# Joining the weighing with the next half group's scores, norms and stores by half groups, and a new load order, in a planned four-layer graph kernel

## The chip, the cores and the metric

One core of one Trainium2 chip. The metric is the time of one execution in microseconds (us), the median of several on the device. All runs used here of one kernel agree within about 0.2%. TensorE is the matmul engine, DVE the vector engine, ACT the scalar engine, GpSimd (POOL in the profile) the fourth; PSUM is where TensorE writes. "One group" is four pairs of graphs, 512 nodes; there are 16 groups.

## The reference, cut to what matters

```python
# x (128, 64, 256), adj (128, 64, 64) holds 0 and 1 only, nodemask (128, 64); all float32
h = relu(layernorm(x));  x = x + attention_0(h, adj)    # 8 heads; where(adj > 0, scores, -9e15)
h = relu(layernorm(x));  x = x + attention_1(h, adj)    # scores + log(adj + 1e-6)
h = relu(layernorm(x));  x = x + gru(h, adj, nodemask)  # 5 steps, each: m = h @ weight[l]
                                                        # agg = (adj != 0)^T m;  h = GRU(agg, h)
h = relu(layernorm(x));  x = x + gated(h, adj)          # theta, norm by degree, gate, elu
```

## The kernel before

The kernel does not issue its instructions as they are written. Each is recorded with an assumed cost, an engine and its operands; a small planner then fixes the order of every engine's instructions at build time, as a list scheduler with a clock of its own:

```python
AFTER = {"PE": 210, "DVE": 125, "ACT": 45, "POOL": 90, "SP": 2500}   # ns from an end to its user
TO_PE = 120
AHEAD = 1.2
...
    @contextmanager
    def strand(self, base, span=1.0):       # gives the ops recorded inside keys base .. base + span
...
    def run(self):                          # cut: takes the op that can start first, by key, within
        ...                                 # a horizon of AHEAD; knows the port that DVE and GpSimd share
```

Attention works on half a group. Its two narrow blocks on TensorE use 64-wide tiles of the array: the scores (s) and the weighing of the values (o). They are recorded far apart:

```python
        def scores():                       # 8 matmuls, stationary operand 128x64
            for i in range(2):
                ps = pss[i].tile.rearrange("p (h k) -> p h k", h=HEADS)
                for c in range(2):
                    for gp in range(2):
                        t0 = i * P + gp * NODES
                        nc.tensor.matmul(ps[gp * NODES : (gp + 1) * NODES, c * 4 : (c + 1) * 4, :],
                                         qT[:, c, t0 : t0 + NODES], k_exp[:, c, :, t0 : t0 + NODES],
                                         start=True, stop=True)
        pe(1970, scores, [qT, k_exp], pss, holds=es)
        # cut: softmax on DVE, ACT, GpSimd; transposes of the weights (aT)
        pe(1180, weigh, [v_exp, *aTs], [po], holds=[oT])   # 16 matmuls, stationary operand 128x64
        # cut: oT copied by DVE, y = oT @ Wo, x += y
```

The recurrence (five steps, matmuls gb, gc, nb, nc and agg) is a chain; TensorE fills its waits with the attention of the next group ("front") and the last layer of the group before ("back"). That rests on these strands:

```python
    for g in range(n_groups):
        xt, h, ht, A, adjT, norm = held
        with plan.strand(g - 0.1, 1.05):
            h = gru(h, ht, A, str(g))
        if g + 1 < n_groups:
            with plan.strand(g + 0.1):
                held = front(g + 1)
        with plan.strand(g + 1.1, 0.6):
            back(g, xt, h, adjT, norm)
```

## Time and profile before

| | before |
|---|---|
| time, median | 2737.6 us (2737.26 to 2738.7, 3 runs) |
| profiled span, granted clock | 2738.0 us, 0.994 |
| TensorE idle from 200 to 2590 us | 2.2 us |
| one group in the steady state | 164.69 us |

The last row is how I read the steady state: each group has one group of four transposes named adjT, and in the list of matmuls by time they start at 755.43, 920.11, 1084.81, 1249.49 us, so 164.69 us apart.

### The profile page before, as it was taken

The numbers are of one execution on the slowest core, as the hardware profiler recorded it, in microseconds if no ns is written. First come the engines' busy times: TensorE is split into PE (matmuls) and PEld (weight loads), VectorE is DVE, ScalarE is ACT, GpSimd is POOL, SyncE is SP. The second block draws the span as 40 slices with busy tenths as digits, with TensorE's granted clock in tenths as the row PEclk, the third lists the DMA queues.
The fourth block names the chain that finished last, engine by engine and source line by source line (L and its number), as shares of the span: only waits on it lengthen the run. The fifth ranks groups of instructions, "written<-read, shape, count | busy, mean of one in ns | idle before, by whom it ended". The sixth has DMA issues, their size and how long they took to land.

```text
span 2738.0 us, 41144 instructions
## 1 busy us (share of the span) xinstructions
PE 2687.4 (98%) x15593; PEld 2244.2 (82%) x15593; DVE 1977.9 (72%) x4401; ACT 1410.1 (51%) x2743; POOL 764.0 (28%) x820
## 2 busy tenths in 40 slices
PE   8899999999999999999999999999999999999996
PEld 5688888888888888888888888888888888888884
DVE  4676687777777777777777777777777777777766
ACT  4445455455555545455455555555455455554542
POOL 5332232232332323232232332322222232322211
PEclk9999999999999999999999999999999999999998
DMA  3000000000000000000000000000000000000000
GB/s 122 5 1 1 1 17 5 1 16 1 17 5 10 8 1 20 1 16 1 1 20 1 17 1 8 13 1 16 1 16 1 1 17 1 16 1 1 9 8 8
DMA packets 31401, 27.70 MB, mean 10 GB/s; under 512 B 9234, under 2 KB 30948, under 8 KB 31204
## 3 DMA queue, kind: packets, MB, share of 16 engines
q1 hardware_dynamic: 31204, 25.08, 2.9%
q8 instruction: 123, 2.02, 0.3%
q14 instruction: 74, 0.61, 0.1%
HBM read 16.69 MB, written 8.39 MB: 9 GB/s over the span
## 4 chain that ended last, share of the span: by engine, by line
PE 95%; DVE 3%; ACT 1%; issue 1%; DMA 0%; POOL 0%; SPq 0%; POOLq 0%; DVEq 0%; ACTq 0%
PE gb L679 20%; PE gc L679 15%; PE nb L679 10%; PE nc L679 8%; PE agg L712 5%; PE s L528 4%; PE y L584 4%; PE gate L930 4%; PE q L473 4%; PE v L504 4%; PE k L473 4%; PE o L573 2%; PE hT L419 2%; PE aT L557 2%; PE lnT L419 2%; PE f L924 2%
## 5 line engine op out<-in xcount | busy, mean ns | idle before, releaser
L782 POOL TENSOR_TENSOR s0n<-h,s0n 128x512 f32<-128x512 f32 x80 | 108.1, 1352 | 718.8 <-ACT s0n L779 718.8
L679 PE MATMUL gb<-Th,w_hh 128*128 128x256 f32 x960 | 247.9, 381 | 1.8 <-DVE s22g L743 1.1
L679 PE MATMUL gb<-Ta,gv 128*128 128x256 f32 x960 | 247.7, 380 | 0.9 <-DVE Ta L722 0.8
L551 POOL TENSOR_TENSOR e<-e,ssum 128x512 f32<-128x512 f32 x128 | 139.5, 1101 | 307.8 <-DVE ssum L550 305.3
L743 DVE TENSOR_TENSOR s0g<-gc,ug 128x512 f32<-128x512 f32 x80 | 55.3, 692 | 215.5 <-PE gc L679 215.5
L679 PEld LDWEIGHTS gb<-Th,w_hh 128*128 128x128 f32 x960 | 176.8, 190 | 32.8 <-issue 10.0
L679 PEld LDWEIGHTS gb<-Ta,gv 128*128 128x128 f32 x960 | 178.2, 190 | 24.4 <-DVE Ta L722 1.7
L650 POOL TENSOR_TENSOR Th<-h 128x256 f32<-128x256 f32 x160 | 134.4, 844 | 216.5 <-PE nb L679 79.4
L717 ACT ACTIVATE agg<-agg 128x512 f32<-128x512 f32 x160 | 95.3, 595 | 182.0 <-DVE Ta L722 127.1
L650 POOL TENSOR_TENSOR Th<-h,Th 128x256 f32<-128x256 f32 x160 | 123.4, 771 | 233.7 <-DVE h L796 120.9
L772 ACT ACTIVATE s0g<-s0g,b_rz 128x512 f32<-128x512 f32 x160 | 110.6, 714 | 138.6 <-DVE s0g L743 138.5
L712 PEld LDWEIGHTS agg<-adjblk,ht 128*128 128x128 f32 x1280 | 164.3, 191 | 10.0 <-ACT ht L424 3.7
L712 PE MATMUL agg<-adjblk,ht 128*128 128x128 f32 x1280 | 169.8, 276 | 0.0
L679 PE MATMUL gc<-agg,gv 128*128 128x256 f32 x640 | 165.3, 381 | 0.0
L679 PE MATMUL gc<-h,w_hh 128*128 128x256 f32 x640 | 164.5, 379 | 0.0
L409 POOL TENSOR_TENSOR rstd<-pw,mhalf 128x4 f32<-128x4 f32 x64 | 65.4, 1022 | 300.9 <-DVE pw L408 300.9
L473 PE MATMUL q<-hT,w_L_gnn_Wq 128*128 128x256 f32 x512 | 146.0, 388 | 1.6 <-DVE hT L427 1.6
L446 DVE TENSOR_SCALAR xn<-x,mv,rstd 128x256 f32<-128x256 f32 x256 | 109.8, 461 | 51.0 <-POOL rstd L409 42.8
L679 PE MATMUL nb<-Th,w_hh 128*128 128x256 f32 x480 | 143.0, 380 | 0.0
L679 PE MATMUL nb<-Ta,gv 128*128 128x256 f32 x480 | 142.8, 379 | 0.0
L504 PE MATMUL v<-w_L_gnn_Wv,hT 128*128 128x256 f32 x512 | 138.4, 380 | 0.0
L473 PE MATMUL k<-hT,w_L_gnn_Wk 128*128 128x256 f32 x512 | 137.4, 381 | 0.0
(161 smaller groups left out, 6864.7 us busy)
## 6 DMA issues: line engine op xcount, KB each, us to landing
x<-in_x_dram SPq DMA_DIRECT2D x16, 512.0 KB, 3.8
out_dram<-x SPq DMA_DIRECT2D x16, 512.0 KB, 2.8
adjq<-in_adj_dram SPq DMA_DIRECT2D x8, 256.0 KB, 2.9
gv<-in_L_gnn_weight_dram SPq DMA_DIRECT2D x5, 256.0 KB, 5.6
w_ih<-in_L_gnn_w_ih_dram SPq DMA_DIRECT2D x2, 384.0 KB, 6.0
w_hh<-in_L_gnn_w_hh_dram SPq DMA_DIRECT2D x2, 384.0 KB
w_L_gnn_Wo<-in_L_gnn_Wo_dram SPq DMA_DIRECT2D x2, 256.0 KB, 4.2
w_L_gnn_Wq<-in_L_gnn_Wq_dram SPq DMA_DIRECT2D x2, 256.0 KB
```

The costliest lines, as they stand in the source:

```text
L419: nc.tensor.transpose(ps[:, i * P : (i + 1) * P], src_at(i), ident.tile)
L446: vec2(400, lambda p=p, i=i, xn=xn: nc.vector.tensor_scalar(xn[:, i, :], xt[:, p, :], mv[:, p, 0:1], rstd[:, p : p + 1], op0=ALU.subtract, ...
L473: pe(mm(256), lambda c=c, kc=kc: nc.tensor.matmul(ps[:, c * HALF : (c + 1) * HALF], wt[:, kc, c * P : (c + 1) * P], hT[:, kc, :], start=kc ...
L504: pe(mm(256), lambda i=i, kc=kc: nc.tensor.matmul(pv[:, i * D : (i + 1) * D], hT[:, kc, i * P : (i + 1) * P], w["v"][:, kc, :], start=kc = ...
L528: nc.tensor.matmul(ps[gp * NODES : (gp + 1) * NODES, c * 4 : (c + 1) * 4, :], qT[:, c, t0 : t0 + NODES], k_exp[:, c, :, t0 : t0 + NODES], ...
L551: pool(1090, lambda e=e, z=z: nc.gpsimd.tensor_tensor(e.tile, e.tile, z[:, :, None].to_broadcast(shape), op=ALU.mult), [e, z], [e])
L584: pe(mm(256), lambda i=i, c=c: nc.tensor.matmul(py[:, i * D : (i + 1) * D], oT[:, i, c, :], w["o"][:, c, :], start=c == 0, stop=c == 1), [ ...
L650: pool(790, lambda: nc.gpsimd.tensor_tensor(T[:, i, :], x(), y(), op=ALU.subtract), reads, [(T, i)])
L679: nc.tensor.matmul(bank_[:, col * HALF : (col + 1) * HALF], at(g, n), rhs(), start=first and j == 0, stop=True, skip_group_check=True)
L712: nc.tensor.matmul(ps[:, p * P : (p + 1) * P], ht[:, p, c * P : (c + 1) * P], A[:, p, :], start=True, stop=True)
L772: sca(act(n, 1), lambda k=k, col=col: nc.scalar.activation(wide(g_v, k), src_at(k), AF.Tanh, bias=b_rz[:, col : col + 1], scale=0.5), [src ...
L930: pe(mm(512), lambda kc=kc, s=s, pg=pg, hT=hT: nc.tensor.matmul(pg.tile, hT[:, kc, s], w_th[:, kc, :], start=kc == 0, stop=kc == 1), [hT, ...
```

## The change

Its intent: leave the narrow form of the array less often, by issuing one half's weighing directly ahead of the next half's scores; start sooner, by loading x first; fill the prologue with two groups' attention in turns; shorten the tail by half groups. The diff, cut to its core:

```diff
-            vec(345, ... bn_stats(st[:, p, :], xt[:, p, :]) ...        # norms: four tiles, one power
+    def norm_relu_t(xt, half, dst, access, writes, name, by_token=None):  # two tiles, one power each
...
-            transposed(dst, access, xn, ..., half == 1, writes, relu=True)  # half 0 on DVE, half 1 on ACT
+        transposed(dst, access, xn, ..., True, writes, relu=True)           # both on ACT
...
+        if waiting:
+            weigh_last, reads, po_last, oT_last, finish_last = waiting.pop()
+
+            def both():
+                weigh_last()
+                scores()
+
+            pe(2900, both, [*reads, qT, k_exp], [po_last, *pss], holds=[oT_last, *es])
+            finish_last()
+        else:
+            pe(1970, scores, [qT, k_exp], pss, holds=es)
...
-        pe(1180, weigh, [v_exp, *aTs], [po], holds=[oT])
+        waiting.append((weigh, [v_exp, *aTs], po, oT, finish))     # the last one of a group is flushed
...
-                nc.sync.dma_start(rows.tile[r0 : r0 + n, :], ...)       # bias rows, nodemask
+                nc.scalar.dma_start(rows.tile[r0 : r0 + n, :], ...)
+        plan.add("ACT", 2600, fill_rows, [], [rows], lat=2500)
+        load_x(0)                                                        # ahead of adj and weights
...
-    with plan.strand(-1.0):
-        held = front(0)
+    with plan.strand(-1.0):
+        for g in (0, 0, 1, 0, 1, 0):
+            next(parts[g])                                              # one half-layer each
...
-            with plan.strand(g + 0.1):
-                held = front(g + 1)
-        with plan.strand(g + 1.1, 0.6):
-            back(g, xt, h, adjT, norm)
+            with plan.strand(g - 0.1, 0.9):
+                for _ in parts[g + 1]:
+                    pass
+        with plan.strand(g + 1.1, 0.5):
+            back(g, xt, h, adjT, norm)                                  # itself by halves, stores too
```

## The prediction

> **What bounds the kernel now.** I read the page's busy shares first, then the busy times cut into stretches, then TensorE's matmuls in order of time, then the chain of waits at both ends. From the page of the kernel before:
>
> ```profile
> PE 2687.4 (98%) x15593; PEld 2244.2 (82%) x15593; DVE 1977.9 (72%) x4401; ACT 1410.1 (51%) x2743; POOL 764.0 (28%) x820
> ...
> PE   8899999999999999999999999999999999999996
> ```
>
> TensorE is busy 98%; the next engine, DVE, 72%. The digits say that TensorE's idle time lies in the first two and the last of 40 slices. Busy times in stretches that I chose at events of the trace (first norm transpose, first recurrent step, steady state, last group's recurrence, tail), TensorE alone (busy us, count, granted clock, DMA share, GB/s):
>
> ```profile
> 0.00:13.06 13.06, 2.42 (x5) 1.00 0.66 210
> 13.06:120.40 107.34, 97.24 (x549) 0.95 0.18 55
> 120.40:200.00 79.60, 76.20 (x452) 1.00 0.00 1
> 200.00:2590.00 2390.00, 2387.83 (x14032) 1.00 0.02 7
> 2590.00:2699.40 109.40, 104.02 (x506) 1.00 0.02 6
> 2699.40:2738.00 38.60, 19.67 (x56) 0.72 0.04 14
> ```
>
> From 200 to 2590 us TensorE is idle 2.2 us of 2390. There nothing but less TensorE work shortens the program; faster DVE, GpSimd or DMA is worth nothing. All other idle time is 10.6 + 10.1 + 3.4 + 5.4 + 18.9 = 48.4 us, 1.8% of the span, and much of it (the first load, the last chain) can't go. So even a perfect removal of idle time would stay under 2%, and that limits this prediction more than anything else.
>
> The second source is inside the busy time. TensorE's matmuls in order of time in the steady state (start, us, line, count; each matmul of the source stands as two):
>
> ```profile
> 731.75 0.60 PE L557 MATMUL aT<-ident,e 128*128 128x128 f32 x4
> 732.18 1.06 PE L712 MATMUL agg<-adjblk,ht 128*128 128x128 f32 x8
> 733.17 1.95 PE L528 MATMUL s<-kexp,qT 128*64 128x256 f32 x16
> 735.05 0.65 PE L557 MATMUL aT<-ident,e 128*128 128x128 f32 x4
> 735.54 0.60 PE L679 MATMUL nb<-agg,gv 128*128 128x256 f32 x2
> 735.97 1.03 PE L679 MATMUL gc<-agg,gv 128*128 128x256 f32 x4
> 736.93 1.15 PE L573 MATMUL o<-aT,vexp 128*64 128x64 f32 x32
> 738.01 0.70 PE L679 MATMUL nc<-agg,gv 128*128 128x256 f32 x2
> 738.55 1.03 PE L504 MATMUL v<-w_L_gnn_Wv,hT 128*128 128x256 f32 x4
> ```
>
> Read the starts, not the durations. Four matmuls of 256 columns normally take 0.86 us from start to start and two take 0.43. The four (gc) ahead of the weighing (o) take 736.93 - 735.97 = 0.96, and the two (nc) after it 738.55 - 738.01 = 0.54. So 0.10 us is lost on entering and 0.11 on leaving. For the scores (s): agg takes 0.99 where eight take 0.89 elsewhere (0.10 lost), and the transposes after it 0.49 where four take 0.43 (0.06 lost). Only s and o have a 128*64 stationary operand; all else has 128*128. None of this shows as idle.
>
> **What the Trainium skill says.** "TensorEngine Tiling (Array Packing)", Key Properties: "Changing tiling mode (not just tile) drains the TensorE". The trace agrees in sign and gives the size, about 0.1 us per change. "TensorE: Matmul & The Clock Gate", Part 1 (What's actually happening), says that an idle array falls to half clock until it has been busy for a window of about 3.4 us. The trace agrees: the first eight q matmuls took 3.62 us where a warm eight take 1.89, and in 75 to 100 us, after waits of 2.6 us and less, the mean granted clock was 0.81. "DMA: Bandwidth & Descriptors", Anatomy of one DMA, gives about 2.0 us fixed cost. Here the first load, 256 KB of adj issued at 0.73, let DVE start at 3.69: 2.96 us, no contradiction.
>
> **Part 1, weighing joined with the next scores.** The instruction orders of the two builds show 128 narrow blocks on TensorE before (64 s, 64 o, never adjacent), and 80 after: 48 joined, 16 s and 16 o alone. (A group has four half-layers; the last weighing of each group is flushed alone.) Counts of matmuls per kind are the same. Each join removes one leaving and one entering: 0.06 to 0.11 plus 0.10, say 0.20 us. 48 x 0.20 = **9.6 us**. As TensorE is full where most of them lie, I count all of it. The planner's own constants imply 0.25 per join (12 us).
>
> **Part 2, x first.** Before, x was the ninth load issued (4.29 us) and DVE's statistics began at 9.48; then 1.73 us of statistics for four tiles, 0.17 for adding epsilon, 1.03 for the power on GpSimd, 0.42 for the first normalisation, first transpose at 13.06:
>
> ```profile
> 9.48 1.41 DVE L439 BATCH_NORM_STATS2 st<-x 128x6 f32<-128x256 f32 x4 [2.92 <-DMA x<-in_x_dram]
> ...
> 11.53 1.03 POOL L409 TENSOR_TENSOR rstd<-pw,mhalf 128x4 f32<-128x4 f32 x1 [6.58 <-DVE pw L408]
> ...
> 13.06 1.22 PE L419 MATMUL lnT<-ident,xn 128*128 128x128 f32 x4 [4.36 <-DVE xn L446]
> ```
>
> After, half of x (256 KB) is the first load on its queue, so by the adj load's example it is there at about 3.7. Statistics of two tiles take about 0.9, power and its input 1.3, two normalisations 0.73: first transpose at about 6.7, **6.3 us earlier**. The bias rows move to ACT's queue: six issues of 0.23 to 0.64 us (2.1 us) and 2.1 to landing put the small transpose of them at about 5.2, as before, so it does not hold the first norm. Weights wanted first (Wq, Wk) follow x directly.
>
> **Part 3, two groups' attention in turns, weight folding spread.** Between 13 and 120 us TensorE idles 10.1 us and loses 0.05 x 107 = 5.4 us to the lower clock: 15.5 us in all. The largest waits are a normalisation (1.9 and 0.7), a softmax of group 0 that nothing filled (2.6) and a key placement behind it (0.4). Group 1's scores now stand between group 0's, and the GpSimd folds (20 + 4 adds of 1 us) move behind. But the new order runs dry of folding matmuls after the second layer's first half, and GpSimd stays busy. I count 40%: **6 us**, and 1.5 of the 3.4 us idle in 120 to 200.
>
> **Part 4, the tail by halves.** Today the last group's norm waits for both halves of h. After, the half that is ready first (h at 2703.5 by today's clock) goes through transposes (1.1 us), two residuals, statistics of two tiles and its own power while the other half's last update runs. On DVE these are interleaved, so I get the first transposes at about 2709.9 for 2712.07 today. From there DVE sets the pace: a tile takes 0.48+0.42+0.48+0.43+0.43+0.29+0.42+0.42 = 3.37 us of it and today's tiles follow each other by 3.07 to 3.49, which the change does not alter. So 2.2 us, and about 0.5 for a last store of 256 instead of 512 KB: **2.7 us**.
>
> **Part 5, what it adds.** Norms by halves double the powers: 64 more of 1.02 us on GpSimd (764 to about 830 of 2738 us) and move 64 PSUM evictions of 0.68 us from DVE to ACT as 0.59. Both engines have room and nothing of it is on the path in the steady state: 0. Stores and loads in halves move the same bytes in 32 more transfers, hidden: 0. The joined block needs three PSUM banks of four at once and both operands ready; I add 1.5 us for waits that this makes.
>
> Sum: 9.6 + 6.3 + 6 + 1.5 + 2.7 - 1.5 = 24.6 us. 2737.6 - 24.6 = **2713.0 us**, 0.9% less.
>
> **Rivals.** (a) The join becomes a wait: scores can't start before the last weighing's transposed weights are evicted, and three banks of four are held. For it: the order is fixed at build time, so a misplaced block stalls TensorE each time; 48 stalls of 0.4 us take back the whole of part 1 and half of part 3: about 2726. Against it: the same planner left 2.2 us idle in 2390, so its costs are good. (b) The load order starves the fold: the folding matmuls now stand between the first q, k and v and need the GRU weights by about 10 us; 2.5 MB must land first, and the first 25 us moved 280 GB/s (9 us). A late one costs 2 to 4 us and a cold clock: 2717. (c) The prologue works fully: all 15.5 us of part 3 and 12 us of joins return: about 2701. (d) GpSimd becomes the limit in the prologue, as it now has 24 folds, 12 norms and the softmax scalings of two groups: part 3 gives nothing, 2719. I hold the middle for likelier than either end.
>
> **Range and chances.** The rivals span 2701 to 2726; I widen by a little: 2700 to 2726. A gain of over 2% needs under 2682.8, 54.8 us less: more than all idle time plus the joins' 9.6 could give with a tail that must keep most of its 39 us; 3%. A loss of over 2% needs 55 us of new waits on a full TensorE: 1%.
>
> **What would show it.** Joins: o followed at once by s in the matmuls' order, without 0.1 us around them, and the steady stretch shorter by 0.6 us per group with as little idle time. Start: first norm transpose near 6.7. Prologue: idle and clock loss up to the first recurrent step down from 15.5 to about 9. Tail: last recurrent matmul to end 36 instead of 38.6. Wrong if: TensorE's waits on ACT's aT or on a bank grow by over 5 us in the steady stretch, the fold matmuls wait on a DMA, or a join saves other than 0.2 us.

## More of the kernel before

The few waits of that stretch, as the view of waits has them (waiting matmul, what it waited for: us in total, times, longest):

```profile
PE q L473 <- DVE hT L427: 0.8, 1, 0.8
PE nb L679 <- DVE h L427: 0.8, 1, 0.8
PE gate L930 <- DVE oT L579: 0.7, 1, 0.7
```

None of these three repeats: they belong to the first and last groups.

## The result, and the profile after

The changed kernel takes 2727.13 us (2725.76 to 2728.55, 4 runs) against 2737.43 in the same rounds: a ratio of 0.9962, 95% interval 0.9944 to 0.9979, and 10.3 us less where 24.6 were predicted, and 1.1 us above the top of the range given. (A ratio is the mean time of one kernel's runs over that of the other's runs of the same rounds, so not quite the ratio of the medians quoted.) The four runs fall in two clusters, 2725.8 twice and 2728.5 twice; the profiled run is of the faster one, span 2724.0, so the profiles differ by 14.0 us where the medians differ by 10.3.

The page of the changed kernel, busy shares and TensorE's digits in 40 slices:

```profile
PE 2671.2 (98%) x15593; PEld 2245.0 (82%) x15593; DVE 1965.4 (72%) x4402; ACT 1436.6 (53%) x2808; POOL 762.2 (28%) x883
...
PE   8999999999999999999999999999999999999997
```

TensorE's busy time fell by 16.2 us with the same 15593 matmuls, and yet the time fell by less. TensorE alone in stretches cut at the same events as before (first norm transpose, first recurrent step, steady state, last recurrent matmul):

```profile
0.00:9.56 9.56, 0.37 (x1) 1.00 0.81 232
9.56:118.50 108.94, 102.79 (x640) 1.00 0.19 59
118.50:200.00 81.50, 79.76 (x506) 1.00 0.00 1
200.00:2590.00 2390.00, 2373.83 (x13923) 1.00 0.02 7
2590.00:2689.30 99.30, 96.20 (x471) 1.00 0.02 6
2689.30:2724.00 34.70, 18.27 (x57) 0.82 0.05 16
```

Against before: the start is 3.5 us shorter; the prologue idles 6.2 us instead of 10.1 and its recorded clock is full instead of 0.95 (the record starts late: the first eight q matmuls, at 11.47 us, still take 3.59 us where a later eight take 1.89, and the view shows 1.00 for them as it does in before); the stretch to 200 us idles 1.7 instead of 3.4; the tail takes 34.7 instead of 38.6. But from 200 to 2590 us TensorE idles **16.2 us instead of 2.2**. That is the surprise. The same view of waits for this stretch:

```profile
PE hT L441 <- DVE h L836: 8.8, 25, 0.5
PE gb L719 <- ACT agg L757: 3.4, 2, 2.0
```

The first repeats 25 times, twice in nearly every group: the transposes of h for the next step wait for the last of DVE's updates of h. The second is two waits of the first group's recurrence (1.4 and 2.0 us at 217 and 247 us). The adjT transposes now start at 725.44, 890.69, 1055.85, 1221.10 us, 165.25 and 165.16 apart in turn: **165.21 us a group on average, 0.52 more than before**, although each group has three joins. The joins themselves are there, in the list of matmuls by time (start, us, line, count):

```profile
790.29 1.11 PE L719 MATMUL gc<-agg,gv 128*128 128x256 f32 x4
791.33 1.15 PE L606 MATMUL o<-aT,vexp 128*64 128x64 f32 x32
792.31 1.90 PE L531 MATMUL s<-kexp,qT 128*64 128x256 f32 x16
794.14 0.70 PE L719 MATMUL nc<-agg,gv 128*128 128x256 f32 x2
```

From o to s are 0.98 us where a lone o takes 1.08 to the next start, from s to nc 1.83 where a lone s takes 1.88, and one entering and one leaving of about 0.1 are gone. Summed over one group, the narrow blocks with what is lost at their edges take 12.42 us instead of 13.28: 0.29 us per join.

At the start, all engines in order of time:

```profile
3.53 0.60 ACTq L337 DMA_DIRECT2D rows<-in_nodemask_dram  x1
3.53 0.75 DVE L461 BATCH_NORM_STATS2 st<-x 128x6 f32<-128x256 f32 x2 [0.53 <-DMA x<-in_x_dram]
...
8.27 0.37 PE L384 MATMUL pc<-ident,rows 82*128 82x82 f32 x1 [8.27 <-DMA rows<-in_nodemask_dram]
8.68 0.24 DVE L386 COPY cols<-pc 128x82 f32<-128x82 f32 x1 [3.32 <-PE pc L384]
...
9.10 0.73 DVE L467 TENSOR_SCALAR xn<-x,mv,rstd 128x256 f32<-128x256 f32 x2
```

The statistics of x begin at 3.53, as predicted. But the last of the small loads on ACT's queue is issued at 3.53 and the transpose (pc) of what it brings can start only at 8.27; DVE's copy of that stands ahead of the first normalisation (xn) in the fixed order, and so DVE idles 3.3 us with the data of xn at hand.

What the 0.53 us wait looks like from inside, all engines, one group:

```profile
727.16 0.42 DVE L817 SCALAR_TENSOR_TENSOR s21n<-s21n 128x256 f32<-128x256 f32 x1
727.39 0.78 POOL L690 TENSOR_TENSOR Th<-h,Th 128x256 f32<-128x256 f32 x1 [2.75 <-DVE h L826]
727.50 0.82 DVE L830 TENSOR_SCALAR s21g<-s21g 128x256 f32<-128x256 f32 x1
728.13 0.77 POOL L690 TENSOR_TENSOR Th<-h 128x256 f32<-128x256 f32 x1
728.24 0.95 DVE L936 TENSOR_SCALAR adjblk<-adjblk 128x512 f32<-128x512 f32 x1
...
731.67 0.42 DVE L836 TENSOR_TENSOR h<-s21n 128x256 f32<-128x256 f32 x1
```

DVE never rests here. L830 takes 0.82 us where its median over the run is 0.29, and L936 (the comparison of the adjacency block with zero) 0.95 where it took 0.42 in every group of before. Both run beside GpSimd's subtractions. The Trainium skill, "SBUF — State Buffer", section "SBUF: two separate sides", says that DVE and GpSimd arbitrate for one port pair, as an exclusive lock held for a whole instruction. The trace agrees: 0.53 us more on each of two instructions, while GpSimd's take their usual 0.77. And it is no chance: of L830's 80 executions 34 start while a GpSimd instruction runs, and 33 of these take 0.81 us or more; the other 46 all take 0.28 or 0.29. But the lock is not new either: the same operation of before (L790) is lengthened in 33 of 80 executions too. What differs is where the two engines meet. Between L830 and the last update of h (L836) the order also holds a residual, two statistics with their aggregates and a normalisation of the next group's front.

### The profile page after: what moved, and what is told of

Same layout as the page of the kernel before. It is cut to its first block, busy times and chain, and to the rows that moved or that the text cites. A ratio compares the mean times of both kernels' runs of the same rounds, so it can differ in the third digit from the quotient of the medians.

```text
span 2724.0 us, 41462 instructions
## 1 busy us (share of the span) xinstructions
PE 2671.2 (98%) x15593; PEld 2245.0 (82%) x15593; DVE 1965.4 (72%) x4402; ACT 1436.6 (53%) x2808; POOL 762.2 (28%) x883
## 4 chain that ended last, share of the span: by engine, by line
PE 88%; DVE 8%; ACT 2%; issue 1%; DMA 0%; POOL 0%; DVEq 0%; ACTq 0%
PE gb L719 17%; PE gc L719 16%; PE nb L719 8%; PE nc L719 8%; PE agg L752 5%; PE s L531 4%; PE v L551 4%; PE gate L978 4%; PE q L496 4%; PE k L496 3%; PE y L618 3%; PE o L606 2%; PE hT L441 2%; PE f L972 2%; PE aT L590 2%; PE lnT L441 2%
## 5 line engine op out<-in xcount | busy, mean ns | idle before, releaser
L822 POOL TENSOR_TENSOR s0n<-h,s0n 128x512 f32<-128x512 f32 x80 | 102.1, 1276 | 377.1 <-ACT s0n L819 377.1
L762 DVE TENSOR_TENSOR Ta<-agg,agg 128x256 f32<-128x256 f32 x160 | 67.4, 421 | 144.6 <-ACT agg L757 144.5
L719 PEld LDWEIGHTS gc<-agg,gv 128*128 128x128 f32 x640 | 119.8, 190 | 26.5 <-ACT agg L757 9.3
L690 POOL TENSOR_TENSOR Th<-h 128x256 f32<-128x256 f32 x160 | 122.9, 773 | 65.0 <-DVE h L826 47.3
L719 PEld LDWEIGHTS gc<-h,w_hh 128*128 128x128 f32 x640 | 115.3, 190 | 22.3 <-issue 5.5
```

What stands on the lines that cost most here:

```text
L690: pool(790, lambda: nc.gpsimd.tensor_tensor(T[:, i, :], x(), y(), op=ALU.subtract), reads, [(T, i)])
L719: nc.tensor.matmul(bank_[:, col * HALF : (col + 1) * HALF], at(g, n), rhs(), start=first and j == 0, stop=True, skip_group_check=True)
L822: pool(n * 1.85 + 320, lambda: nc.gpsimd.tensor_tensor(b_(), hh2(), a_(), op=ALU.subtract), [*hp, n_v], [n_v])
```

## The experiments

Fifteen kernels ran. The theories, as they were named on the way: **A**, the new positions of the strands put the filler matmuls in the wrong places; **B** (later also called H), the join itself makes TensorE wait; **C**, the norms by halves, with all their evictions on ACT, delay what TensorE needs; **D**, no part of the change does, but any order that the planner fixes anew has waits that its clock does not see, and before's order was one with hardly any. E, F and G are named in the run that they belong to. All results are correct except joinonly's. The time of before was 2736.95 to 2737.85 us.

### strands: the strands' positions undone

```diff
-            with plan.strand(g - 0.1, 0.9):
+            with plan.strand(g + 0.1):
-        with plan.strand(g + 1.1, 0.5):
+        with plan.strand(g + 1.1, 0.6):
```

> The changed kernel with the planner's time bases of the two filler streams put back (next group's attention 0.1 later and over 1.0 instead of 0.9 of a group, layer 3 over 0.6 instead of 0.5); joins, halves and start stay. In the steady state the changed kernel's period is 165.22 us per group where the kernel before has 164.69, though its three joins save 0.29 us each (0.87); 0.73 us of new waits of hT on DVE's h and about 0.65 of waits hidden in the spacing eat it. Theory A (the earlier filler streams put attention's DVE work before the recurrence's last update and leave 7.6 us of filler matmuls in the last recurrent layer for 19.2 before): those waits go, period about 163.9, time 2727.1 - 13 x 1.3 = about 2711. Rival B (the join itself makes the waits) and rival C (norms by halves, evictions all on ACT): period stays at 165.2, time 2727 within 3.

Measured 2774.68 us, ratio 1.0137. The period is 167.8 us. The waits for h did go, as A said (one of 0.8 us is left), but the two largest waits are new ones, for the normalisations of the front and back (15.9 and 7.0 us in all). So A's cure falls: the old positions make this kernel slower. As the whole order is a new one, it is not shown that any order needs the new positions.

### nojoin: each weighing alone

The changed kernel with the weighing recorded where before had it, all else as changed (the helper for the last weighing and its call go too).

```diff
-        waiting.append((weigh, [v_exp, *aTs], po, oT, finish))
+        pe(1180, weigh, [v_exp, *aTs], [po], holds=[oT])
+        finish()
```

> The changed kernel with each weighing issued alone, as before; all else stays. Measures the join. Theory A: waits of hT on h stay at about 0.7 us per group and the narrow blocks cost 48 x 0.29 = 14 us more: about 2741, slower than the kernel before. Rival B: the waits go with the join (1.4 us per group) and the spacing of the narrow blocks returns (0.87 per group): about 2720. By my prediction's 0.20 per join it would be 2727 + 9.6 = 2737.

Measured 2743.04 us, ratio 1.0023. It is 15.9 us more than with the join, 0.33 per join, near A's number. But A expected the waits for h to stay, and they vanish; others of nearly the same sum come in their place (transposes of the weights for GpSimd's e, 4.6 us; y for DVE's oT, 3.4), and the period is 166.45. So waits are no mark of the join. This too is another order, so the 0.33 is not the join alone; jwide and jnarrow below keep the order.

### rows: the true landing time of the bias rows told to the planner

```diff
-        plan.add("ACT", 2600, fill_rows, [], [rows], lat=2500)
+        plan.add("ACT", 2600, fill_rows, [], [rows], lat=5500)
```

> The changed kernel with one number changed: the planner is told that the bias rows come 5.5 us after their issue, not 2.5, so it places the first norm's transposes ahead of the small transpose of the rows, which in the changed kernel held TensorE to 8.27 and the first norm to 9.56. First norm transposes at about 6.7, first q at 8.7 for 11.47: 2.8 us less, 2724.3, if the start is worth what it moves; unchanged steady state. If later waits in the prologue swallow it (loads, GpSimd): 2727.

The first norm transpose starts at 6.16 us instead of 9.56 and the first scores at 22.38 instead of 24.05, yet the time is 2726.52 us, 0.6 less. In its profile the mean clock falls to 0.91 between 230 and 250 us (0.51 from 246.4 to 249.8), behind the two waits for agg, and from the second adjT transpose to the third it takes 306.2 us instead of the 304.6 of the changed kernel's profiled run. The changed kernel's own slower cluster (2728.5) has a lower mean clock too, 0.997 for 0.998. I take it for the same drop; no profile of a run of that cluster was kept, so this is argued.

### joinonly and joinonly2: before with the join alone

Only within a layer, 32 joins. In joinonly the flush at the end of a layer came after the recording of the next layer's norm, which read an unfinished x: a wrong result. joinonly2 is joinonly with the flush moved ahead of that norm:

```diff
         for layer in range(2):
+            if layer:
+                flush()
             hTs, dst_of = halves(f"{g}_{layer}")
```

> The kernel before with the join alone, where its norms by whole groups allow it: within a layer, so 32 joins, 32 s and 32 o alone. At 0.29 us per join 9.3 us less, 2728.1, and steady state as free of waits as before, if theory A is right (the join costs no waits). Rival B: new waits in every group of 0.7 us and more eat it: 2737 or more. By the 0.20 of the prediction: 2731.

> The kernel before with only the join, inside a layer (32 joins, the last weighing of each layer flushed ahead of the next layer's norm); this mends the earlier run, whose flush came after the norm and gave a wrong result. At 0.29 to 0.33 us per join the joins alone would give 9.3 to 10.6 us: 2727 to 2728. Theory D (any other plan brings waits of some tenths of a us per group in a full TensorE): idle of TensorE from 200 to 2590 us rises from 2.2 to 8 or more, the flush ahead of the norm makes it worse, and the time is 2733 to 2745. Rival C (the halves and the start of the change, not the join, bring the waits): idle stays under 4 us, period under 164.3, 2728.

joinonly took 2736.15 us, ratio 1.0000, with about 10.6 us idle in the steady stretch; its timing stands only as a hint. joinonly2 is correct: 2749.15 us, ratio 1.0046, period 165.97, and 2.0 us idle in each 400 us. The join without the rest of the change loses 12 us. This too is another order, with a flush ahead of a norm, so it does not tell B from D by itself.

### noneq: the comparison with zero left out

In this run D is stated as the one mechanism seen above. adj holds 0 and 1, so the result stays right for these inputs; a kernel for any adj must keep it. The planner still counts it, and the order of all other instructions is the same.

```diff
-        vec2(400, lambda: nc.vector.tensor_scalar(blk.tile, blk.tile, 0.0, None, op0=ALU.not_equal),
-             [blk], [blk])
+        vec2(400, lambda: None, [blk], [blk])
```

> The changed kernel with the in-place comparison of the adjacency block with zero (one DVE operation of 128x512 per group) not issued; adj holds only 0 and 1, so the result must stay right. The order of every other instruction on every engine is the same. Theory D (the joins' gain was eaten because DVE reaches the last update of h late where it has this comparison, 0.95 us there, and the norms' statistics ahead of it, while GpSimd's subtractions run beside it): the hT waits on DVE's h update, 0.53 and 0.20 us per group, fall to under 0.1 each, the period between two groups' adjacency transposes falls from 165.2 to about 164.6, and the time from 2727.1 to about 2717, at least 6 us. Rival E (TensorE waits wherever any engine's order is tight, and this wait only hides the next one): the hT waits go but others of like size come in the same group, the time changes by less than 3 us. Rival F (the comparison is hidden and the wait is ACT's or GpSimd's): nothing changes, 2727.

Measured 2724.75 us (2724.14 to 2725.15), ratio 0.9956: 2.4 us less, not 10. The waits for h, and the stretch of before's picture in this kernel:

```profile
PE hT L441 <- DVE h L836: 4.8, 25, 0.2
```

```profile
729.82 0.77 POOL L690 TENSOR_TENSOR Th<-h,Th 128x256 f32<-128x256 f32 x1 [2.74 <-DVE h L826]
729.93 0.81 DVE L830 TENSOR_SCALAR s21g<-s21g 128x256 f32<-128x256 f32 x1
730.56 0.77 POOL L690 TENSOR_TENSOR Th<-h 128x256 f32<-128x256 f32 x1
730.78 0.83 DVE L832 TENSOR_TENSOR s21n<-s21g,h 128x256 f32<-128x256 f32 x1
```

The 0.53 us wait became 0.2. It was 0.95 us of DVE work taken away, but the lock found another victim: the next DVE instruction, 0.41 us in the changed kernel, now takes 0.83 beside GpSimd's second subtraction. From L830's start to the end of L836 it is 4.25 us instead of 4.59, 0.34 less, and the period fell by exactly that: 164.87. So it is shown that DVE work ahead of h's update makes this wait, at 0.34 us of the 0.6 a group and 2.4 us of the 10 that I expected; a run without the lock itself was not made. F (the wait is not DVE's) is refuted. E's number (under 3 us) came true but not its mechanism: no other wait of TensorE appeared. In the time, 14 periods of 0.34 would be 4.8 us; in this profile the drop of the clock near 250 us and a start 1.1 us later took part of it back.

### bahead and aahead: the same constant of the planner changed on both kernels

```diff
-AHEAD = 1.2
+AHEAD = 1.1
```

> The kernel before with one constant of the planner changed (its look-ahead factor 1.2 to 1.1), so the work is the same and only the order differs. Theory D (the order of before is one whose small waits were tuned away; any other order has them): period from 164.7 up to 165.2 or more, steady idle of 200 to 2590 us from 2.2 to over 8, time 2741 to 2752 (the planner's own clock says 8.6 us more). Rival (the kernel before has slack enough that an order by the same planner stays free of waits; then it is the join that brings them): period 164.5 to 164.9, idle under 4 us, time within 4 us of 2737.

> The changed kernel with the same one constant of the planner changed as in the earlier run on the kernel before (look-ahead 1.2 to 1.1; there it cost 6 us). Theory D (the waits belong to an order, not to the join): the period is that of before's 164.69 less 0.87 for three joins plus whatever waits this order has; I expect waits of 0.4 to 1.8 us per group, a period of 164.2 to 165.6, in other places than those of the changed kernel. Theory H (the joins themselves always bring about 1.4 us of waits per group): period 165.0 to 165.4 and the same waits of hT on DVE's update of h, 0.5 and 0.2 us.

The work is the same in each pair, only the order differs. On before: 2743.18 us, ratio 1.0024, period up from 164.69 to 165.26, without any join. My expected mark, idle over 8 us, did not appear (2.4 us): most of its loss is not shown as idle but as start-to-start spacings that are too long (table below). On the changed kernel: 2735.93 us, ratio 0.9993, period 165.15, with other waits (gb for ACT's agg in nearly every group, 0.3 us each, and h at 0.2). The period alone would fit H, the waits do not: the 0.5 us wait for h is gone. Its 8.8 us more than the changed kernel are not of the steady state: the first agg of its third group starts at 432.81 us for 420.95, and its trace has three stretches at half clock before 304 us, 13.6 us together, where the changed kernel's has none.

### aback and bback: another constant changed by the same step

```diff
-        with plan.strand(g + 1.1, 0.5):     # before: 0.6
+        with plan.strand(g + 1.1, 0.55):    # bback: 0.65
```

> The changed kernel with one constant of the planner changed (the span of the last stage's strand 0.5 to 0.55), the same work in another order. The planner's own clock says 1.4 us less. If its clock could be trusted, 2725.7. Theory D: the waits are in other places and of another size, the time anywhere between 2720 and 2740, and the hT waits of 0.53 and 0.20 us per group do not repeat in that form; the comparison of the adjacency block takes 0.42 or 0.95 us according to whether GpSimd works beside it.

> The kernel before with the last stage's strand span 0.6 to 0.65, the same step by which the changed kernel gained 8 us. Theory D with before's order a tuned one: period above 164.69, by 0.2 to 1.2 us, time 2740 to 2755. Rival (the step is simply better for both kernels, and the change was compared at an unlucky value): period under 164.5, time under 2733.

On the changed kernel **2718.85 us**, ratio 0.9934, period 164.29: 8.3 us faster with the same work, the same 48 joins and the same norms by halves. Its comparison with zero takes 0.39 to 0.42 us again in every group, and its waits for h are down from 8.8 us to 2.5:

```profile
PE gb L719 <- ACT agg L757: 3.4, 2, 2.0
PE hT L441 <- DVE h L836: 2.5, 13, 0.2
```

On before, the like step gives 2767.07 us, ratio 1.0105, period 166.5 and 167.8 in turn. So the step is not a better constant as such: it only gives another order. B and H are refuted as stated, since the joins can have a period below before's.

### evict: half of the norms' evictions back on DVE

```diff
-                   f"lnT_{name}", True, writes, relu=True)
+                   f"lnT_{name}", half == 1, writes, relu=True)
```

> The changed kernel with the normalised transposes' first halves evicted by DVE again, as before, instead of all by ACT. Theory C (ACT's 64 more evictions delay its copies of agg, which TensorE then waits for): the wait of gc on agg (0.31 us per group) goes and the period falls by 0.3 or more below 165.2. Theory D (it is only another order, and DVE gets 64 more copies of 0.7 us): period 164.8 to 166, waits elsewhere, the time 2724 to 2740.

Measured 2737.35 us, ratio 0.9998, period 165.97. The wait of gc for agg that C blamed is still there (0.31 us of spacing), and a new one is the largest:

```profile
PE q L496 <- DVE hT L449: 8.7, 12, 0.8
```

So C's cure fails: with half of the evictions on DVE, which is the busier engine, this kernel was 10 us slower, though in another order. The other half of C, the norms by halves, was not taken back alone in any run; but aback has them at a period of 164.29, and joinonly2 has new waits without them, so they neither force the waits nor are needed for them.

### noturn: the first group's attention alone

```diff
     with plan.strand(-1.0):
-        for g in (0, 0, 1, 0, 1, 0):
-            next(parts[g])
         for _ in parts[0]:
             pass
```

> The changed kernel with the first group's attention recorded alone, the second group's behind it as filler of the first recurrence, as before. Theory G (the turns fill the prologue but take half of the second group's attention out of the first recurrence, which then has too little filler): the waits of 1.4 and 2.0 us at 217 and 247 us for ACT's copy of agg go, with the clock drop behind them, and TensorE's idle time from 130 to 400 us falls from about 7 us to under 3; the prologue up to 120 us idles 10 us or more instead of 6, so the time is 2726 to 2733. Rival (the turns are worth what the plan's own clock says, 14.7 us): 2738 to 2743. Rival (the turns are worth nothing and only cost): under 2724.

Measured 2738.45 us, ratio 1.0006. TensorE alone, from 0 to 120 and from 200 to 410 us, of this kernel:

```profile
0.00:120.00 120.00, 99.20 (x559) 0.96 0.23 72
...
200.00:410.00 210.00, 208.43 (x1261) 1.00 0.02 6
```

The changed kernel has 104.66 at clock 1.00 and 206.26 in these. Theory G is right that the turns take filler out of the first recurrence (its two waits of 1.4 and 2.0 us vanish without them, though one of 1.6 us for h comes at 300 us), but the turns win far more than that in the prologue. They are worth 11.3 us here; the rival "14.7" was nearer than mine. About 5.1 us of it is the clock: noturn's trace has 10.2 us at half clock from 81 us on. The period is 165.2, as in the changed kernel, so this run bears on the start alone.

### jwide and jnarrow: the price of leaving the narrow form by itself

On the aback kernel, one small matmul between the weighing and the scores of each of the 48 joined blocks, whose result the scores overwrite: in jwide with a wide stationary operand, in jnarrow with a narrow one.

```diff
                 weigh_last()
+                nc.tensor.matmul(pss[0][:, :NODES], ident.tile, ident[:, :NODES], start=True, stop=True)
+                # jnarrow: pss[0][:NODES, :NODES], ident[:, :NODES], ident[:, :NODES]
                 scores()
```

> The changed kernel with the span 0.55 (2718.9 us) and, between the weighing and the scores of each of the 48 joined blocks, one small matmul with a 128x128 stationary operand and 64 columns, whose result the scores overwrite. Same order of all else. It puts one leaving and one entering of the narrow form back: 0.29 us per join as the spacing of a steady group says, with the small matmul's own 0.06, so the period from 164.29 to about 165.2 and the time to about 2718.9 + 48 x 0.33 = 2735; less where the 0.2 us waits of hT shrink as TensorE comes later.

> The control of the run before: the same small matmul in the same place, but with a 128x64 stationary operand, so the narrow form isn't left. Period up by 3 x 0.06, the time about 2718.9 + 3 = 2722. The difference between the two is 48 times one leaving and one entering: 10 us by the prediction's 0.20 each, 14 by 0.29.

jwide 2743.44 us (ratio 1.0025), jnarrow 2726.47 (0.9959; one of its four runs 2722.29 at a higher clock). jnarrow is 7.6 us above aback where I expected 3: its small matmuls cost 0.11 us each by the period (164.62 for 164.29), twice my estimate, and three of its runs had a granted clock of 0.995 for aback's 0.996. The difference, 17.0 us, is 0.35 us per join; by the periods, 165.83 and 164.62, it is 1.21 / 3 = 0.40. The same joined block in both, jwide first:

```profile
799.03 1.15 PE L607 MATMUL o<-aT,vexp 128*64 128x64 f32 x32
800.11 0.43 PE L541 MATMUL s<-ident 128*128 128x64 f32 x2
800.48 1.95 PE L531 MATMUL s<-kexp,qT 128*64 128x256 f32 x16
802.35 0.70 PE L720 MATMUL nc<-agg,gv 128*128 128x256 f32 x2
```

```profile
794.34 1.15 PE L607 MATMUL o<-aT,vexp 128*64 128x64 f32 x32
...
797.26 0.70 PE L720 MATMUL nc<-agg,gv 128*128 128x256 f32 x2
```

From o to nc are 3.32 us in jwide, 2.92 in jnarrow and 2.81 in aback. So the whole 0.40 lies at the join and none of it in waits behind it: the late starts, counted as in the table below, are equal in the three kernels. It is more than the 0.29 of the spacings, and part of it may be the small matmul itself: its two weight loads take 0.19 us each in jwide and 0.14 in jnarrow, which these runs cannot separate from the change of form. So a join is worth 0.29 us by the spacings, and 0.35 to 0.40 is an upper mark. In jwide against jnarrow all of it reached the time.

### backrows: aback and rows together

The only two edits are those shown above (0.55, and 5500).

> A candidate to beat both: the changed kernel with the last stage's strand span 0.55 (2718.9 us when run alone) and the bias rows' load told to the planner as 5.5 us to landing instead of 2.5, which moves only the small transpose of them behind the first norm transpose. The latter alone gave the first norm transpose at 6.16 instead of 9.56 and the first scores 1.67 us earlier. If the two add: 2716.5 to 2718. If the start is again given back (a clock drop of 1.7 us at 230 to 270 us, behind the two waits of 1.4 and 2.0 us there): 2718.5 to 2719.5.

Measured **2716.18 us** (2715.42 to 2717.30, 5 runs), ratio 0.9926, interval 0.9913 to 0.9938. First norm transpose 6.68, first scores 22.26 us against aback's 25.01, and here the start's gain arrives. It beats before by 21.5 us and the changed kernel by 10.9, with no work changed against the latter.

### All periods on one account

For one group of each kernel: what the narrow blocks take with their edges, and what the other matmuls' starts are late (sum of all start-to-start spacings over 0.05 us longer than 0.216 us per matmul of 256 columns, 0.110 of 128, 0.430 of 512, idle included, lost records left out).

| kernel | narrow blocks | late starts | sum against before | period measured, against before |
|---|---|---|---|---|
| before | 13.28 | 0.30 | 0 | 164.69 |
| changed | 12.42 | 1.71 | +0.55 | 165.21, +0.52 |
| noneq | 12.42 | 1.39 | +0.23 | 164.87, +0.18 |
| aback | 12.42 | 0.78 | -0.38 | 164.29, -0.40 |
| bahead | 13.28 | 0.80 | +0.50 | 165.26, +0.57 |

The spacings of a group add up to its period, so this is bookkeeping and no test of a cause; it closes within 0.07 us. What it shows is that the joins give the same 0.86 a group in every kernel that has them, while the late starts go from 0.30 to 1.71 and are as large without joins (bahead 0.80) as with them (aback 0.78).

## Why the prediction was wrong

- **The bound: right.** TensorE is 98% busy before and after.
- **The joins, "0.06 to 0.11 plus 0.10, say 0.20 us": too small.** 0.29 by the spacings, and at most 0.35 to 0.40 by jwide and jnarrow. The prediction left out that o and s themselves are 0.05 to 0.10 shorter when they follow each other. 48 of them are about 14 us, not 9.6.
- **The waits: the step that failed.** "Both engines have room and nothing of it is on the path in the steady state: 0" and "I add 1.5 us for waits that this makes". Measured: late starts grew by 1.41 us in every group, some 18 us over the 13 groups of the steady state, which is all that the joins gave and more. The engines had room on average, 72% and 28%; in one stretch of 5 us DVE had none, where two engines met at a shared port. That stretch makes the wait of 0.53 us, which moves the next start by 0.69; the rest of the 1.41 has other places.
- **The argument that led there** is the reason against rival (a): "the same planner left 2.2 us idle in 2390, so its costs are good". bahead and bback show before's planner with one constant moved: 6 and 29 us slower. The 2.2 us were a property of one order, not of the planner's costs. Rival (a) itself had the right number (2726) by a wrong mechanism: it named the evicted weights and the banks; the waits are for h and agg.
- **The start, 6.3 us: 3.5.** Failed step: the landing of the bias rows put "the small transpose of them at about 5.2, as before, so it does not hold the first norm". It came at 8.27 and did hold it, through the fixed order; rows shows 6.16 without that. And a start moved forward is not all won: rows' 3.4 us gave 0.6 us in the median.
- **The prologue, 6 and 1.5 us: too small.** "I count 40%". Idle and clock together gave 9.3, then 1.7; the clock stayed full. noturn puts the turns at 11.3 us in all. Not foreseen: the two waits in the first recurrence, 3.4 us, with a clock drop of 1.7 us in some runs.
- **The tail, 2.7 us: 3.9.** The right mechanism, a little too small: the first transposes come 9.9 us behind the last recurrent matmul instead of 12.7.
- **GpSimd "764 to about 830" us: 762.** The 128 power operations on two tiles each take 92 us together where the 64 on four tiles took 65, so 27 us more and not 65, and other GpSimd operations got shorter. It did not matter for the result.
- **The sum.** The parts above give 3.5 + 9.3 + 1.7 + 3.9 = 18.4 us won outside of the full stretch. Twelve steady groups (from the third group's first agg to the fifteenth's) took 1982.1 us instead of 1976.3, 5.8 lost; as the profiles differ by 14.0, 19.8 were won in the rest. The parts do not add up exactly: work moved between the stretches (2.05 us of bias matmuls stood ahead of before's first transpose and come after it now), and the last group's recurrence idles 3.1 us instead of 5.4. The median gain of 10.3 has half its runs in the slower cluster.

Not settled: why the late starts that are not shown as idle (0.31 us from agg to gc, for one) come about in each order; why the planner, whose clock knows the shared port, lets the two engines meet there; and whether an order without waits exists for the changed work. aback's 0.78 was found with one step of one constant, and each kernel was seen in two or three orders of its own work only.

## What to carry to other kernels

When a schedule is fixed at build time and the bounding engine is full, its near-zero idle time belongs to that one order: any edit can bring a new one, here from 0.9 us a group less (aback) to 2.4 more (bback), as much as the edit itself. So judge an edit at several orders of the same work, read the steady period and not only idle time, and look for the place where an engine that is "28% busy" blocks another for 0.5 us ahead of the one instruction that the full engine waits for. A small cost taken away may only pass the wait for the lock on to the next instruction.

## What the Trainium skill lacked or had wrong

- "TensorEngine Tiling (Array Packing)" says that a change of mode drains TensorE but gives no size: here about 0.10 us on entering and 0.06 to 0.11 on leaving the 64-wide form, and 0.29 us for each pair of changes saved between o and s, their own shorter time included.
- "SBUF — State Buffer" has the lock of DVE and GpSimd right; the runs add the size on this kernel's instructions: a DVE operation of 128x256 went from 0.29 to 0.82 us, one with two inputs from 0.41 to 0.83, one of 128x512 from 0.42 to 0.95, beside GpSimd subtractions of 0.77 (33 of the 34 executions of L830 that start under a GpSimd instruction, none of the other 46).
- "TensorE: Matmul & The Clock Gate", Part 1 (What's actually happening), has the clock fall to half after an idle window of about 3.4 us. Here 3.4 us at half clock, 1.7 us lost, followed a wait of only 2.0 or 2.1 us in the first recurrence, in seven of the nine profiles that have this wait (rows: 0.51 from 246.4 to 249.8 us) and not in the other two (the changed kernel and jwide).
- I found on no page how much of a wait the idle time of the profile leaves out: a shown wait of 0.53 us moved the next start by 0.69, one of 0.20 by 0.36, so 0.16 more each. That is how much longer a record of 256 columns is (0.38 us) than the step to the next start (0.216).
- "DMA: Bandwidth & Descriptors" gives no time for a small load among large ones of another queue: here one of 32 KB issued at 3.53 us on ACT's queue, while 256 KB loads of SyncE's queue were under way, let its reader start only at 8.27, 4.7 us later; in before the same load, issued at 2.97 on SyncE's queue, let it start at 5.25.
